# Attention kernel: a copy ahead of a softening, value products behind a second product, a fourth pair begun with the third

## The chip, the cores and the metric

The kernel runs on one core of a Trainium2 chip. The metric is device time in microseconds (us) of one execution, given as the median of several runs. Times in the text are us if nothing else is said, and times inside a stage count from the start of the profiled span.

## What is computed

The input is eight images of 256 channels and 1024 positions. The first layer is attention with eight heads; the second is attention of a token with all tokens of its image, followed by a mixture of eight experts. The change touches the attention of the second layer, for each image (batch) once:

```python
def _L1_attn_ref(x, W):                       # x: layer-normed tokens, 8 x 1024 x 256
    xa = jnp.einsum('bnd,ed->bne', x, W)
    scores = jnp.einsum('bne,bme->bnm', xa, x)
    attn = jax.nn.softmax(scores, axis=-1)
    y = jnp.einsum('bnm,bmd->bnd', attn, x)
    return y

# --- layer 0 ---
x = _L0_conv_ref(x, L0_conv_w_qkv, L0_conv_b_qkv, L0_conv_w_out, L0_conv_b_out)
# --- layer 1 ---
t = _to_tokens(x)
t = t + _L1_attn_ref(_ln_t(t), L1_attn_W)
t = t + _L1_ffn_ref(_ln_t(t), L1_ffn_router_w, L1_ffn_w1, L1_ffn_b1, L1_ffn_w2, L1_ffn_b2)
```

Layer 0 also needs, for the batch that comes next, its value projection `v` (eight blocks of 128 tokens by 512) and its first queries and keys. The kernel computes part of these inside the second layer's attention of the batch before.

## The kernel before

All work is in float32. The batches run one after the other: `layer0`, then `attend`, then routing; batches 0 to 6 are sent through their experts together, batch 7 at the end by itself (`dense`). For batch 7 `attend` runs beside the gathering of the experts' results (`others.tick`), which puts additions on DVE and transfers on the queues.

**The scores in `attend`** are a 1024 x 1024 matrix of eight row blocks of 128. They are computed by a scheme of Strassen's kind, in four pairs of row blocks: pair k makes blocks k and k + 4 with seven products of 128 x 128 by 128 x 512 in place of eight. `Pair.product` (L761) is one product, two records in the trace. Each pair has a PSUM tile of two banks (`big`, three of these in a pool): the left half `x`, the right half `v`; and one bank `z` from the pool `acc` of two banks, which the mixes' results (`py`) also use.

The steps of a pair, in the order of the program:

- `__init__`: first product into `x`; `first`, a copy of it to SBUF on ACT (L744); second product into the other half, `v`; a product into `z`; on DVE an addition of `v` (L771), which also keeps a running minimum.
- `middle`: a product accumulated into `x`; its copy `second` (L754); another one into `x`, which must wait for that copy; its copy `third` (L756); an addition of `z` on DVE.
- `rest`: two closing products, and then for the even block an addition (nmax) and the softening, an exponential on ACT over 1024 columns (L795); for the odd block a maximum on DVE (L800) and two exponentials on ACT (L804, L812). Pair 1 does the odd block first.

In the text the products of `middle` are called the pair's second and third product, as each is accumulated into `x` after the first.

**Turning and mixing.** The mix of a softened block with the tokens (`mix`, L861, 16 records of 128 x 256) needs the block transposed. `turn_now` does it on TensorE (first and last block). `turn` does it for the six others: a transpose of 32 x 32 squares on DVE (L833), and then the 16 groups of squares go to their places, eight by copies on ACT (32 x 256, L844) and eight by DMAs of 32 KB from the SP queue. The list `behind` holds back each half of them until a given copy of a later pair has been issued. `mix` ends with an addition on DVE (L870) that empties the bank `py`.

**The fill.** `fill(place)` calls `Begin.at` at named places of `attend` and of what follows (`norm 1`, `normed 1`, `last weights`, `last products`, `norm 2`, `normed 2`); each call makes one block of the next batch's value projection (`values(1)`, two products of 0.86 us in the trace's starts, L408, then a bias addition on DVE, L416). For batch 7 `fill` is another function, which does something at `last products` only.

**What sets the order.** A scheduler at build time puts each engine's instructions in a fixed order, from the program's order, the data dependencies and the `tc.issue_after` marks; it knows a PSUM tile as a whole, which is why a few places declare that there is no dependency between banks. On the chip each engine works through its list in order and waits at semaphores. The order of the program at the end of `attend` is: pairs 0 and 1 to their `middle`, `rest` of both, `turn_now` of block 0, pair 2 begun, mix 0, `middle` of pair 2, mix 1, `rest` of pair 2, pair 3 begun, mix 2, `middle` of pair 3, mix 3, `rest` of pair 3, and the mixes 4 to 7.

Of the kernel before, what the change touches and what calls it, by code (L numbers as in the profile page):

```python
# [19 lines left out]
def kernel(  # L20
# [23 lines left out]
    nc = tc.nc  # L44
# [48 lines left out]
    def acc(name):  # L93

        return ps_acc.tile([P, 512], F32, tag="acc", name=name)
# [54 lines left out]
    for e in range(E):  # L150
# [43 lines left out]
        fill=0.0,  # L194
# [135 lines left out]
    evicted = {}  # L330
# [54 lines left out]
    class Begin:  # L385
# [36 lines left out]
        def at(self, place):  # L422

            if place == "norm 1":
                self.project(True)
            elif place == "norm 2":
                with tc.issue_after(evicted["mixed"].ins):
                    self.project(True)
            self.values(1)

        def all(self):
            for _ in range(3):
# [245 lines left out]
    def attend(b, t1, fill, tick=nothing):  # L678
# [13 lines left out]
        HALF = S // 2  # L692
        xa = one.tile([P, NCC, NH2, HALF], F32, tag="xa", name=f"xa_{b}")
        mixes = one.tile([P, 7, HALF], F32, tag="res", name=f"mixes_{b}")
        b11, b12, b21, b22 = (nT[:, e, ts(n, HALF)] for e in range(2) for n in range(2))
        t1_, t2_, t3_, t4_ = (mixes[:, i, :] for i in range(4))
# [4 lines left out]
        a11, s3_, a12, a22 = (xa[:, e, n, :] for e in range(2) for n in range(2))  # L701
        s1_, s2_, s4_ = (mixes[:, 4 + i, :] for i in range(3))
# [27 lines left out]
        class Pair:  # L730

            def __init__(self, k):
                self.k = k
                both = big(f"ps1_{b}_{k}")
                self.x, v = both[:, :HALF], both[:, HALF:]
                self.z = acc(f"ps1z_{b}_{k}")
                self.ex = [homes[EX[2 * k + h]] for h in range(2)]
                self.low = [
                    small.tile([P, 1], F32, tag=f"nlow{h}", name=f"nlow_{b}_{k}_{h}")
                    for h in range(2)  # L740
                ]
                self.left = self.ex[0][:, :HALF]
                self.product(self.x, a11, b11, True)
                self.first = nc.scalar.copy(self.left, self.x)  # L744
                second = self.product(v, a12, b21, True)
                tc.declare_no_dep(second.ins, self.first.ins, reason="the other bank")
                self.product(self.z, s1_, t1_, True)
                self.add(self.left, v, 3.0e38, self.low[0])

            def middle(self, behind=None):  # L750
                far = self.ex[1][:, HALF:]
                with tc.issue_after(behind.ins) if behind else nullcontext():
                    self.product(self.x, s2_, t2_, False)
                self.second = nc.scalar.copy(self.ex[0][:, HALF:], self.x)  # L754
                self.product(self.x, s3_, t3_, False)
                self.third = nc.scalar.copy(far, self.x)  # L756
                self.add(far, self.z, 3.0e38, self.low[1])
                return self
# [23 lines left out]
            def rest(self, behind=None):  # L782
                k = self.k
                self.product(self.z, s4_, b22, False)
                self.product(self.x, a22, t4_, False)
                nmax, ssum = [], []
                for h in range(2):
                    nmax.append(small.tile([P, 1], F32, tag="nmax", name=f"nmax_{b}_{2 * k + h}"))
                    ssum.append(small.tile([P, 2], F32, tag="ssum", name=f"ssum_{b}_{2 * k + h}"))
                ex0, ex1 = self.ex  # L790

                def even():
                    tick(("max", 2 * k), self.add(ex0[:, HALF:], self.z, self.low[0], nmax[0]))
                    with tc.issue_after(behind.ins) if behind else nullcontext():
                        nc.scalar.activation(  # L795
                            ex0, ex0, AF.Exp, bias=nmax[0], scale=-1.0, accum_out=ssum[0][:, 0:1]
                        )

                def odd():
                    last = nc.vector.tensor_scalar(  # L800
                        scrap, self.x, -1.0, self.low[1], ALU.mult, ALU.min, accum_out=nmax[1]
                    )
                    tick(("max", 2 * k + 1), last)
                    nc.scalar.activation(  # L804
                        ex1[:, :HALF],
                        self.x,
                        AF.Exp,
                        bias=nmax[1],
                        scale=1.0,
                        accum_out=ssum[1][:, 0:1],  # L810
                    )
                    nc.scalar.activation(  # L812
                        ex1[:, HALF:],
                        ex1[:, HALF:],
                        AF.Exp,
                        bias=nmax[1],
                        scale=-1.0,
                        accum_out=ssum[1][:, 1:2],
                    )

                for half in (odd, even) if k == 1 else (even, odd):
                    half()
                return [(2 * k, ex0, ssum[0][:, 0:1], None), (2 * k + 1, ex1, *self.halves(ssum[1]))]
# [4 lines left out]
        def turn(i, ex, behind=None):  # L828


            at_sq, at_aT = SQ_AT[i]
            sq = homes[at_sq]
            nc.vector.transpose(sq, ex)  # L833
            if at_aT is None:
                aT = two.tile([P, S], F32, tag="tr", name=f"aT_{b}_{i}")
            else:
                aT = homes[at_aT]
            to = aT.rearrange("p (m a q) -> p a m q", a=NQ, q=SQ)
            since = sq.rearrange("p (m k q) -> p k m q", k=NQ, q=SQ)
            for a in range(NQ):  # L840
                for k in range(NQ):
                    move = nc.sync.dma_start if (a + k) % 2 else nc.scalar.copy
                    with tc.issue_after(behind[a * 2 // NQ].ins) if behind else nullcontext():
                        move(to[ts(k, SQ), a], since[ts(a, SQ), k])  # L844
            return [aT[:, ts(m, P)] for m in range(NT)]
# [10 lines left out]
        def mix(at, aT, ssum, more):  # L856
            i = BLOCKS[at]
            ahead = fill("last products") if at == NT - 1 else None
            py = acc(f"py_{b}_{i}")
            for m in range(NT):  # L860
                evicted["mixed"] = nc.tensor.matmul(  # L861
                    py[:, :D], aT[m], n1[:, m, :], start=(m == 0), stop=(m == NT - 1)
                )
            rs = small.tile([P, 1], F32, tag="rs1", name=f"rs1_{b}_{i}")
            if more is not None:
                nc.vector.tensor_add(rs, ssum, more)
                ssum = rs
            nc.vector.reciprocal(rs, ssum)
            with tc.issue_after(ahead.ins) if ahead else nullcontext():
                mixed = nc.vector.scalar_tensor_tensor(  # L870
                    t2[:, i, :], py[:, :D], rs, t1[:, i, :], ALU.mult, ALU.add
                )
            tick(("mixed", at), mixed)
# [3 lines left out]
        def turned(at, ex, ssum, more, behind=None):  # L877
            return at, turn(at, ex, behind), ssum, more

        pairs = [Pair(0).middle(), Pair(1).middle()]  # L880
        first, second = pairs[0].rest(pairs[1].third)
        second = turned(*second)
        third, fourth = pairs[1].rest()
        now = turn_now(0, first[1])
        pairs.append(Pair(2))
        mix(0, now, *first[2:])
        pairs[2].middle(evicted["mixed"])
        third = turned(*third, (pairs[2].first, pairs[2].second))
        fourth = turned(*fourth, (pairs[2].second, pairs[2].second))
        mix(*second)  # L890
        fifth, sixth = pairs[2].rest()
        pairs.append(Pair(3))
        mix(*third)
        pairs[3].middle()
        fifth = turned(*fifth, (pairs[3].second, pairs[3].second))
        sixth = turned(*sixth, (pairs[3].third, pairs[3].third))
        mix(*fourth)
# [436 lines left out]
    class Results:  # L1334
# [96 lines left out]
        def tick(self, place, behind=None):  # L1431
            added, sent, stored = self.PLACES.get(place, (0, 0, 0))
            if place == ("max", 0):
                self.scored = behind
            if added:
                with tc.issue_after(behind.ins):
                    for _ in range(added):
                        self.add()
            for _ in range(sent):
                self.gather(behind)  # L1440
            for _ in range(stored):
                if self.whole:
                    b, total, n = self.whole.pop(0)
                    store(b, total, n)
# [135 lines left out]
    for b in range(B):  # L1580
# [18 lines left out]
        def fill(place):  # L1599

            nonlocal norm
            others.tick(place)
            if place == "last products":
                norm = Norm(t1, one.tile([P, NT, D], F32, tag="xa", name=f"n2_{b}"), 1e-5, f"f{b}")
                return norm.blocks(0, NT - 1)
# [46 lines left out]
```

## Time and profile before

| | us |
|---|---|
| median of 3 runs | 2337.22 |
| lowest and highest run | 2333.23, 2338.61 |
| the profiled execution, as timed | 2328.95 |
| its span, first to last instruction | 2327.1 |
| ACT busy | 1163.0 (50%) |
| DVE busy | 1554.5 (67%) |
| mean granted TensorE clock | 0.992 |
| scores' products, L761, one record | 0.592, 448 records |
| mixes, L861, one record | 0.379, 1024 records |

The attention stage of `attend` begins at 189.4, 432.1, 672.3, 912.7, 1153.2, 1394.1, 1634.2 and about 2100 us for batches 0 to 7. The stages of batches 1 to 6 have the same order of instructions and all but the same idle times; batch 0 and batch 7 differ. Records of matmuls overlap, so that the distance between two starts says more of what a product takes than its length does: 0.86 us for a product of two records.

TensorE's idle time in these stages, by what ended it, as the trace lists it (us, times, longest):

```
PE ps L761 <- ACT home L754: 8.2, 14, 1.6
PE py L861 <- DVE t L870: 3.8, 5, 0.9
PE ps L761 <- ACT home L756: 3.4, 2, 2.8
PE ps L761 <- DVE nlow L771: 2.4, 8, 1.1
PE pa L851 <- ACT home L804: 1.7, 2, 0.9
```

A line reads: the engine and the line that waited, the tile that it writes, then the engine, tile and line that released it.

### The profile page before, as it was taken

To read this page: it belongs to the slowest core of one execution; us is meant where nothing else is said; L and a number is where in the kernel's file an instruction comes from. 1 tells how busy PE (TensorE), PEld (TensorE's weight loads), DVE (VectorE), ACT (ScalarE), POOL (GpSimd) and SP (SyncE) were. 2 spreads that over 40 slices of the span, in tenths; PEclk is the share of its full clock that TensorE was granted. 3 is DMA by queue.
4 is the path that set the end of the run, shared out by engine and by line. 5 is a ranking of instruction groups with operands and counts; after the bars stand their busy time and mean duration, and the time that the engine had idled before them with its cause. 6 is when DMAs were issued, how large, how long until landed. Compare 5 with 4: busy or idle time off the path is not lost.

```text
span 2327.1 us, 37989 instructions
## 1 busy us (share of the span) xinstructions
PE 2261.6 (97%) x13059; PEld 1216.1 (52%) x13059; DVE 1554.5 (67%) x4029; ACT 1163.0 (50%) x2138; POOL 410.7 (18%) x392
## 2 busy tenths in 40 slices
PE   9999999999999999999999999999999999998798
PEld 3345533563456335643564355435553488884565
DVE  5775687567855786578657775777568766436655
ACT  3664466456635663656365646465646622225211
POOL 0000012000200020003000200020002135545563
PEclk9999999999999999999999999999999999999899
DMA  8995201020103010201020101100111157765574
GB/s 294 385 386 154 68 17 39 9 56 13 44 2 62 8 49 1 46 19 53 3 46 19 49 8 29 36 26 13 23 42 42 49 145 192 192 199 145 154 210 113
DMA packets 278759, 200.10 MB, mean 86 GB/s; under 512 B 189576, under 2 KB 232232, under 8 KB 276776
## 3 DMA queue, kind: packets, MB, share of 16 engines
q1 hardware_dynamic: 252472, 139.14, 21.2%
q0 software_dynamic: 25008, 58.01, 7.8%
q8 instruction: 104, 1.70, 0.3%
q10 hardware_dynamic: 1088, 0.52, 0.1%
q14 instruction: 87, 0.71, 0.1%
HBM read 108.88 MB, written 110.90 MB: 94 GB/s over the span
## 4 chain that ended last, share of the span: by engine, by line
PE 80%; ACT 5%; DVE 4%; issue 4%; DMA 3%; POOL 3%; SPq 1%; another core or an unknown queue 0%; DVEq 0%; ACTq 0%; POOLq 0%
PE po L569 19%; PE psc L492 19%; PE py L861 7%; PE pqk L371 7%; PE pr L671 5%; PE pv L408 4%; PE ps L761 4%; PE ph L1269 3%; PE pe L1295 3%; PE px L708 2%; POOL yk L1391 2%; PE pqk L349 2%; PE ps1z L761 2%; DMA y<-yb 1%; ACT aT L844 1%
## 5 line engine op out<-in xcount | busy, mean ns | idle before, releaser
L533 ACT ACTIVATE ex<-psc,nmax 128x1024 f32<-128x1024 f32 x512 | 570.0, 1114 | 299.8 <-DVE scrap L516 217.4
L492 PE MATMUL psc<-qk,qk 64*64 64x512 f32 x4096 | 575.8, 593 | 3.8 <-ACT ex L533 3.5
L569 PE MATMUL po<-ex,vs 64*64 64x512 f32 x4096 | 570.6, 591 | 3.6 <-DVE vs L549 2.6
L516 DVE TENSOR_SCALAR_CACHE_REDUCE scrap<-psc,nmax 128x512 f32<-128x512 f32 x512 | 384.2, 750 | 160.3 <-PE psc L492 133.6
L507 DVE TENSOR_REDUCE nmax<-psc 128x1 f32<-128x512 f32 x512 | 350.1, 684 | 9.3 <-PE psc L492 9.3
L492 PEld LDWEIGHTS psc<-qk,qk 64*64 64x64 f32 x4096 | 180.4, 132 | 279.2 <-ACT ex L533 132.6
L569 PEld LDWEIGHTS po<-ex,vs 64*64 64x64 f32 x4096 | 176.5, 132 | 275.6 <-DVE vs L549 82.1
L1081 POOL DMA_INDIRECT rows<-n,d_at x112 | 109.0, 973 | 661.1 <-DVE nmax L507 660.8
L1008 POOL TENSOR_TENSOR t<-t,n 128x2048 f32<-128x2048 f32 x8 | 36.3, 4535 | 875.5 <-DVE n L263 875.5
L371 PE MATMUL pqk<-xT,wqkv 128*128 128x512 f32 x384 | 171.2, 599 | 0.0
L861 PE MATMUL py<-n,spare 128*128 128x256 f32 x512 | 122.0, 394 | 11.3 <-DMA out_dram<-oT 3.8
L336 ACT ACTIVATE qk<-pqk,b_qks 128x512 f32<-128x512 f32 x124 | 85.6, 690 | 86.7 <-PE pqk L371 77.6
L1391 POOL DMA_INDIRECT yk<-y,yat x112 | 111.3, 994 | 76.4 <-issue 28.4
L371 PEld LDWEIGHTS pqk<-xT,wqkv 128*128 128x128 f32 x384 | 71.0, 190 | 99.9 <-issue 77.0
L408 PE MATMUL pv<-wqkv,xT 128*128 128x512 f32 x256 | 121.5, 599 | 1.5 <-DVE v L416 1.0
L861 PEld LDWEIGHTS py<-n,spare 128*128 128x128 f32 x512 | 100.7, 198 | 38.1 <-issue 23.9
L671 PE MATMUL pr<-wo,res 128*128 128x256 f32 x512 | 111.9, 379 | 0.7 <-ACT res L588 0.7
L844 ACT COPY spare<-home 32x256 f32<-32x256 f32 x256 | 103.0, 402 | 10.0 <-DVE home L833 6.7
L671 PEld LDWEIGHTS pr<-wo,res 128*128 128x128 f32 x512 | 97.2, 190 | 17.7 <-ACT res L588 4.7
L1279 ACT ACTIVATE hb<-ph,wb 128x256 f32<-128x256 f32 x96 | 40.1, 470 | 126.9 <-issue 89.4
L533 ACT ACTIVATION_READ_ACCUMULATOR ex<-psc,nmax 128x1 f32 x512 | 99.1, 194 | 0.0
L870 DVE SCALAR_TENSOR_TENSOR t<-py,rs,t 128x256 f32<-128x256 f32 x64 | 30.5, 476 | 98.0 <-PE py L861 85.3
(256 smaller groups left out, 2939.7 us busy)
## 6 DMA issues: line engine op xcount, KB each, us to landing
rows<-wb SPq DMA_DIRECT2D x7, 8192.0 KB
xr<-rows SPq DMA_DIRECT2D x252, 64.0 KB
y<-yb POOLq DMA_DIRECT2D x63, 256.0 KB
xs<-in_x_dram SPq DMA_DIRECT2D x64, 128.0 KB
spare<-home SPq DMA_DIRECT2D x256, 32.0 KB
out_dram<-oT SPq DMA_DIRECT2D x60, 128.0 KB
xT<-in_x_dram SPq DMA_DIRECT2D x7, 1024.0 KB
sums<-t SPq DMA_DIRECT2D x7, 1024.0 KB
```

Of the source, the lines that this page charges most:

```text
L371: mm = nc.tensor.matmul(pq[:, ts(n, 512)], wqkv[:, cc, t, ts(g, P)], xT[:, cc, ts(n, 512)], start=(cc == 0), stop=(cc == NCC - 1),)
L408: nc.tensor.matmul(pv, self.xT[:, cc, ts(i, P)], wqkv[:, cc, 2, :], start=(cc == 0), stop=(cc == NCC - 1),)
L492: mm = nc.tensor.matmul(pss[at, h][ts(c, DK), ts(n, 512)], k[r, j * P + c * DK : j * P + (c + 1) * DK], q[r, ts(n, 512)], start=True, stop ...
L507: firsts[at, h] = nc.vector.tensor_reduce(nmax, pss[at, h][:, ts(0, 512)], AX.X, ALU.max, negate=True)
L516: seconds[h] = nc.vector.tensor_scalar(scrap, pss[at, h][:, ts(1, 512)], -1.0, nmaxes[at, h], ALU.mult, ALU.min, accum_out=nmax,)
L533: nc.scalar.activation(ex, pss.pop((at, h)), AF.Exp, bias=nmaxes.pop((at, h)), scale=1.0, accum_out=sums[at][:, h : h + 1],)
L569: mm = nc.tensor.matmul(po[n][ts(h, DK), :], vss[at][keys, h, :], exps[at, h][keys, ts(n, 512)], start=(j == 0 and turn == 0), stop=(j == ...
L671: nc.tensor.matmul(pr[:, :C], res[:, g, ts(i, P)], wo[:, g, :], start=(g == 0), stop=(g == NPAIR - 1))
L761: return nc.tensor.matmul(to, stationary[:, ts(self.k, P)], moving, start=start, stop=True, skip_group_check=not start,)
L844: move(to[ts(k, SQ), a], since[ts(a, SQ), k])
L861: evicted["mixed"] = nc.tensor.matmul(py[:, :D], aT[m], n1[:, m, :], start=(m == 0), stop=(m == NT - 1))
L1391: ins = nc.gpsimd.indirect_dma_start(out=self.slot(at)[:, k, :], out_offset=None, in_=self.group.y[:, :], in_offset=bass.IndirectOffsetOnAxis(
```

## The change

It has five parts. The value block made at `last products` is made at a new place, `between`, right behind the third pair's second product (for batch 7 nothing is made there). `middle` is cut in two, `middle` (second product and its copy) and `end` (third product, its copy, an addition). The fourth pair's first two products come right after the third pair is begun, before the first mix, and its copy, its bank `z` and its addition later in `open`. The softening of the second pair's even block is called only after the third pair is begun, so that the third pair's first copy is ahead of it. The third mix stands between the fourth pair's second and third product. And in the turn of block 6 two of the eight DMAs become copies on ACT, so ten copies and six DMAs.

```diff
@@ Begin.at
-            self.values(1)
+            if place != "last products":
+                self.values(1)
@@ class Pair
-                self.x, v = both[:, :HALF], both[:, HALF:]
-                self.z = acc(f"ps1z_{b}_{k}")
+                self.x, self.v = both[:, :HALF], both[:, HALF:]
...
                 self.product(self.x, a11, b11, True)
+                if k < 3:
+                    self.open()
+                else:
+                    self.product(self.v, a12, b21, True)
+
+            def open(self):
                 self.first = nc.scalar.copy(self.left, self.x)
-                second = self.product(v, a12, b21, True)
-                tc.declare_no_dep(second.ins, self.first.ins, reason="the other bank")
+                if self.k < 3:
+                    second = self.product(self.v, a12, b21, True)
+                    tc.declare_no_dep(second.ins, self.first.ins, reason="the other bank")
+                self.z = acc(f"ps1z_{b}_{self.k}")
                 self.product(self.z, s1_, t1_, True)
-                self.add(self.left, v, 3.0e38, self.low[0])
+                self.add(self.left, self.v, 3.0e38, self.low[0])
 
             def middle(self, behind=None):
+                with tc.issue_after(behind.ins) if behind else nullcontext():
+                    mm = self.product(self.x, s2_, t2_, False)
+                self.second = nc.scalar.copy(self.ex[0][:, HALF:], self.x)
+                return mm
+
+            def end(self):
                 far = self.ex[1][:, HALF:]
-                with tc.issue_after(behind.ins) if behind else nullcontext():
-                    self.product(self.x, s2_, t2_, False)
-                self.second = nc.scalar.copy(self.ex[0][:, HALF:], self.x)
                 self.product(self.x, s3_, t3_, False)
@@ Pair.rest, even
                     tick(("max", 2 * k), self.add(ex0[:, HALF:], self.z, self.low[0], nmax[0]))
+                    if k != 1:
+                        self.soften()
@@ turn
-                    move = nc.sync.dma_start if (a + k) % 2 else nc.scalar.copy
+                    away = (a + k) % 2 and (i < 6 or a > 0)
+                    move = nc.sync.dma_start if away else nc.scalar.copy
@@ attend
         now = turn_now(0, first[1])
         pairs.append(Pair(2))
+        pairs[1].soften()
+        pairs.append(Pair(3))
         mix(0, now, *first[2:])
-        pairs[2].middle(evicted["mixed"])
+        between = pairs[2].middle(evicted["mixed"])
+        with tc.issue_after(between.ins):
+            fill("between")
+        pairs[2].end()
...
         fifth, sixth = pairs[2].rest()
-        pairs.append(Pair(3))
-        mix(*third)
-        pairs[3].middle()
+        pairs[3].open()
+        between = pairs[3].middle()
+        with tc.issue_after(between.ins):
+            mix(*third)
+        pairs[3].end()
```

What the scheduler makes of it on TensorE in batches 1 to 6, from the first mix on (s2 and s3 are a pair's second and third product, z3 is the fourth pair's product into its bank z, c the two closing products of a pair, v a value product of 0.86 us, m0 to m7 the mixes, T the transposes of the last block):

```
before: m0  v s2(2) v s3(2)  m1  c(2) z3  m2 s2(3) s3(3)     m3  c(3)    m4 T v v m5 m6 m7
after:  m0  s2(2) v v s3(2)  m1  c(2) z3  s2(3) m2 s3(3)  v  m3  c(3) v  m4 T     m5 m6 m7
```

On ACT, from the second block's turn on (k the copies of 32 x 256, E the softening of the second pair's even block, f, s and t the first, second and third copy of a pair, X the exponentials of the third pair):

```
before: 8k E f(2) 4k f(3) s(2) 4k 1k t(2) 7k X s(3) 4k t(3) 4k 8k
after:  8k f(2) E 4k s(2) 4k 3k t(2) 5k f(3) X s(3) 8k t(3) 8k
```

On DVE the fourth pair's addition of `v`, which follows f(3), stands ahead of the addition that empties the bank of m1; before the change it stood earlier, ahead of the third pair's addition of `z`. In batch 0 the order after is m0 s2(2) v v s3(2) v, the closing products of the third pair, v, s2(3), s3(3), m1, z3, m2. In batch 7 the order on TensorE is the same before and after. Outside these stages no engine's order changes.

More of the change, by code (lines that the diff above doesn't have):

```diff
@@ L793, in even, with soften @@
                     tick(("max", 2 * k), self.add(ex0[:, HALF:], self.z, self.low[0], nmax[0]))
+                    if k != 1:
+                        self.soften()
+                def soften():
                     with tc.issue_after(behind.ins) if behind else nullcontext():
@@ L797, in even @@
                         )
+                self.soften = soften
                 def odd():
@@ L878, in turned @@
             return at, turn(at, ex, behind), ssum, more
-        pairs = [Pair(0).middle(), Pair(1).middle()]
+        pairs = [Pair(0)]
+        pairs[0].middle()
+        pairs[0].end()
+        pairs.append(Pair(1))
+        pairs[1].middle()
+        pairs[1].end()
         first, second = pairs[0].rest(pairs[1].third)
```

## The prediction

> **What bounds the kernel now.** I read the page's busy times first, then the timeline of one attention stage engine by engine (batch 2, 679 to 739 us; batches 1 to 6 repeat it), then the stretches' clocks.
>
> ```profile
> span 2327.1 us, 37989 instructions
> PE 2261.6 (97%) x13059; PEld 1216.1 (52%) x13059; DVE 1554.5 (67%) x4029; ACT 1163.0 (50%) x2138; POOL 410.7 (18%) x392
> ```
>
> TensorE is busy 97% of the span, so all idle time together is 65.5 us, and only idle time can be won: the edits add and remove no matrix product. TensorE's rows of the stage (start us, length us, engine, line, operation, tiles; in brackets the idle time before it and its releaser; two records are one 512-column product, sixteen are one mix):
>
> ```profile
> 700.28 1.02 PE L408 MATMUL pv<-wqkv,xT 128*128 128x512 f32 x2
> 701.50 1.12 PE L761 MATMUL ps<-mixes 128*128 128x512 f32 x2 [0.19 <-DVE nlow L771]
> 702.46 1.02 PE L408 MATMUL pv<-wqkv,xT 128*128 128x512 f32 x2
> 703.81 1.13 PE L761 MATMUL ps<-mixes,xa 128*128 128x512 f32 x2 [0.33 <-ACT home L754]
> 704.77 3.62 PE L861 MATMUL py<-n,aT 128*128 128x256 f32 x16
> ...
> 709.95 1.02 PE L761 MATMUL ps1z<-mixes 128*128 128x512 f32 x2
> ...
> 714.26 1.02 PE L761 MATMUL ps<-mixes 128*128 128x512 f32 x2
> 716.01 1.13 PE L761 MATMUL ps<-mixes,xa 128*128 128x512 f32 x2 [0.73 <-DMA home<-home]
> ```
>
> ```profile
> 728.19 3.62 PE L861 MATMUL py<-n,spare 128*128 128x256 f32 x16
> 732.45 3.69 PE L861 MATMUL py<-n,spare 128*128 128x256 f32 x16 [0.65 <-DVE t L870]
> ```
>
> Start to start, a product takes 0.86 us (709.09 to 709.95) and a mix 3.45; the first product after a wait takes 0.96 (703.81 to 704.77). By these (the brackets leave out the tail of a product's length, which the next one overlaps) the stage loses 0.36 at 701.50, 0.49 at 703.81, 0.89 at 716.01 and 0.81 at 732.45, with three restarts of 0.10 and one of 0.08. Why, is in the rows of ScalarE (ACT), VectorE (DVE) and the SP queue:
>
> ```profile
> 698.33 1.15 ACT L795 ACTIVATE home<-home,nmax 128x1024 f32<-128x1024 f32 x1
> 699.48 0.56 ACT L744 COPY home<-ps 128x512 f32<-128x512 f32 x1
> 700.89 1.65 ACT L844 COPY spare<-home 32x256 f32<-32x256 f32 x4 [0.84 <-DVE home L833]
> ...
> 703.17 0.59 ACT L754 COPY home<-ps 128x512 f32<-128x512 f32 x1
> ```
>
> ```profile
> 699.61 1.25 DVE L833 STREAM_TRANSPOSE home<-home 128x1024 f32<-128x1024 f32 x1 [3.37 <-ACT home L795]
> 700.78 0.65 DVE L771 CUSTOM_DVE_ANT_0 home<-home,ps 128x512 f32<-128x512 f32 x1
> ```
>
> ```profile
> 718.09 12.80 SPq L844 DMA_DIRECT2D spare<-home  x16
> ```
>
> The third pair's second product (701.50) waits for the add of 700.78, which waits behind a transpose, and that behind the softening of 698.33. The third product waits for the copy of 703.17. The fourth pair's third product (716.01) comes right behind its second, with only the copy between. The seventh mix (732.45) starts 1.56 us after the SP queue has issued the last of 16 DMAs (718.09 + 12.80 = 730.89); the DVE instruction that the row names empties another bank.
>
> **The change part by part,** walked through with these durations along each engine's order as built, batch 2 first.
>
> *Copy ahead of the softening.* ScalarE comes free at 698.33 as now. The copy goes first, the softening starts 0.61 later (a copy before an activation, 226.37 to 226.98 in batch 0), at 698.94; the add is done by about 699.7, so the second product starts when TensorE is free: 700.28 instead of 701.50, 0.36 of idle time gone. But the softening is 0.61 late, and its transpose (start to start 1.28) comes at 700.22, the four 32x256 copies at 701.50; they stand ahead of the pair's second copy, which starts at 703.15 (4 x 0.41) and ends at 703.73. The third product starts at 703.78, 0.03 earlier than now. The value product (1.72, both halves) now lies behind the second product and ends at 702.86, so the wait is 0.92: the stall has moved, not gone. Gain 0.03.
>
> *The new queue.* In the built order three, not one, of the next 32x256 copies precede the pair's third copy, then five more, and the first copy of the fourth pair, formerly at 702.69, comes only behind all of these: 703.76 + 4 x 0.41 + 3 x 0.41 = 706.65 third copy, 707.26 + 5 x 0.41 = 709.32 fourth pair's first copy, done 709.90. On DVE the fourth pair's add waits for it (709.94 to 710.55) and, behind that in the queue, the emptying of the second mix's bank (L870 for py_4, 708.43 now): 710.55 to 711.03. The fourth pair's third operand product (ps1z_3, 709.95 now) takes that bank. Without a wait it would start at 703.78 + 0.96 + 3.45 + 0.86 + 0.86 = 709.91; it starts at about 711.08. **New wait 1.17, with the restart 1.27.** What is late behind it: the nmax of the third pair (711.6), its softening, the fifth mix's transposes; these are needed from 724 on and ready by 722.
>
> *Fourth pair begun with the third; mix between its products.* The third mix (3.45) now lies between the fourth pair's second and third product, whose chain (1.02 + copy 0.58) is hidden under it: 0.89 + 0.10 gone. If that mix were not there the 0.99 would be back.
>
> *Value products.* Two single products take places behind the third and fourth pairs instead of before the sixth mix: same 1.72 us, no cost, but they no longer cover the wait for the seventh mix's turned block.
>
> *Two DMAs become two copies in that turn.* ScalarE does 10 x 0.41 = 4.1 us instead of 3.3; the SP queue issues 6 instead of 8 (5.2 us now from 725.7 to 730.89, 0.65 each). In the walk TensorE has the fourth pair's closing products at 721.54, the fifth mix at 724.12, the seventh mix at 731.89. The softening starts at 723.39, the transpose at 724.95 behind the bias addition of the value product, the copies at 726.2 to 730.3, the DMAs land at 726.2 + 6 x 0.65 + 1.56 = 731.7. No wait, slack 0.2: 0.89 gone. With eight DMAs there would be one of 1.1.
>
> Batch 2: -0.03 - 0.99 - 0.89 + 1.27 = **-0.64**; the next stage's first product starts at 738.79 instead of 739.43. Batch 1 gives -0.67. In batches 3 to 6 the wait before the seventh mix is 0.90 where it is 0.65 here, but the landing is 0.26 later too and eats the slack: -0.8 each. Together -4.5; bounds: nothing won at the seventh mix, -4.5 + 5.3 = +0.8; new wait half as long, -4.5 - 3.8 = -8.3.
>
> *Batch 0* is ordered differently: the fourth pair's second and third product come before the second mix. The same walk gives waits of 0.92, 1.68, 1.49, 0.83 and 0.79, with restarts 6.4, where the trace has 5.1 in the same places (0.19 to 1.56 shown, plus restarts). **+1.3**, bounds 0 and +2.
>
> *Batch 7* has no value products. Its second copy, bound by the queue of ScalarE, comes at 2130.58 for 2130.08: +0.5. Its last turned block's eight DMAs are issued in 8.95 us, 1.12 each, and TensorE idles 2.17 before the seventh mix; two fewer save between 0 and 2.2. I take 1.0, as in batch 2 most but not all of the 1.3 is won. **-0.5**, bounds -1.7 and +0.5.
>
> Sum: -4.5 + 1.3 - 0.5 = **-3.7 us.** The profiled execution took 2328.95 (span 2327.1), so 2325.2 for one like it; it is 8.3 below the median of the runs shown, 2337.22 (2333.23 to 2338.61). Against the median: **2333.5**, -0.16%.
>
> One possible cost, the clock. Batch 0 idles 1.56 us before a product, and its stretch keeps clock 1.00 (last but two columns: PEclk, DMA share, GB/s follow the busy times):
>
> ```profile
> 222.00:228.00 6.00, 3.87 (x10) 1.25 (x9) 2.12 (x6) 5.81 (x13) 0.00 (x0) 1.00 0.32 51
> ...
> 2130.00:2140.00 10.00, 8.89 (x25) 5.42 (x24) 8.42 (x22) 6.58 (x15) 6.03 (x6) 0.83 0.80 204
> ```
>
> In batch 7 the stretch behind idle times of 1.05 and 0.68 has 0.83, which costs 10 x 0.17 = 1.7 us. I take the first: the new waits are of its size. By the row of batch 7 seven stages would cost 12 us and the sum would be +8. [...]
>
> **The rivals.** (1) *The new wait is shorter or absent*, because the bank is freed earlier than walked (DVE's add takes the copy sooner, the small copies overlap). For: the walk chains 21 ScalarE instructions, and 0.05 too much in each is 1.0. Against: the queues are in order, and 0.41 is steady over all 256 of them. Half gone: -7.5, 2329.7; all: -11.3, 2325.9. (2) *The gain at the seventh mix doesn't come*: another DMA, or the ten copies, land last. Slack is 0.2, so 0.25 us on the landing removes a part and 1.1 the whole: -3.7 + 5.3 = +1.6, 2338.8; half, 2336.2. (3) *Slower*: the new wait at ps1z_3 is longer. Without it batches 1 to 6 win 12.1, batches 0 and 7 lose 0.8; at 1.9 us with restart per batch nothing is left, from 2.7 it is slower by 0.2%. If the emptying of the bank came also behind the third pair's nmax and maximum (0.75 + 0.75 on DVE), it is 2.8: +5.5, 2342.7. For: it stands in the same queue; against: in the built order these two come behind it. (4) The change doing nothing is excluded, as the built order differs in every stage.
>
> **How the numbers follow.** A measurement of this kernel can tell about 0.2% (4.7 us) from no change. Forecast 0.60, its own range 2330 to 2337 with the spread of the runs (2.7 either way); rival 1 0.20, rival 2 0.10, rival 3 0.10. The forecast lies 1 us inside the bound, so of its 0.60 some 0.20 falls beyond it; rival 1 is faster nearly whole: faster 0.40, same 0.49 (0.40 + 0.09 of rival 2), slower 0.11. The range reaches to rival 1's full case and half way to rival 3: 2326.5 to 2340.
>
> **What would show it.** Behind the first mix, the second product without idle time and the third with about 0.9. ps1z_3 with 1.2 of idle time before it, released by DVE L870 of the changed numbering. No idle time between the fourth pair's second and third product, none before the seventh mix. Batch 0 longer by 1.3. Wrong it would be if ps1z_3 starts without a wait, or if the seventh mix still waits for DMAs.

## The result and the profile after

The changed kernel took 2333.59 us (median of 12, 2330.56 to 2340.12), the kernel before beside it 2335.81 (median of 12, 2333.16 to 2338.61): a ratio of 0.9991 with a 95% interval of 0.9982 to 1.0001. That is no change that can be told. The whole of the two profiled spans says the same, 2328.6 for 2327.1, but its stages do not. A stage's length is taken here from the first record of the `px` products of a batch to the first record of what follows the attention, read from the starts in the timelines (the second set is one of the sets of runs below, made on another chip):

```
batch                      0      1      2      3      4      5      6      7   1 to 6
before                 69.26  67.13  67.10  67.36  67.36  67.13  67.92  87.70   404.00
changed                72.64  66.77  66.68  66.70  66.71  66.68  67.69  86.87   401.23
before, second set     69.27  67.14  67.11  67.37  67.37  67.15  67.05  81.09   403.19
changed, second set    70.97  66.79  66.69  66.71  66.70  66.69  67.23  81.95   400.81
```

Batches 1 to 6 won 2.77, batch 7 0.83; batch 0 lost 3.38, and the stretches between the stages, which the change doesn't touch, took 1.73 more in this execution (2.23 of it behind batch 7). So the gain was not won and lost in one place: it is small in each of six stages, and one stage gives it back.

TensorE's timeline of batch 2 in the changed kernel (start, length, engine, line, operation, tiles; in brackets the idle time before and its releaser):

```profile
703.36 1.02 PE L772 MATMUL ps<-mixes 128*128 128x512 f32 x2
704.21 1.88 PE L408 MATMUL pv<-wqkv,xT 128*128 128x512 f32 x4
706.89 1.12 PE L772 MATMUL ps<-mixes,xa 128*128 128x512 f32 x2 [0.79 <-ACT home L761]
...
712.16 1.02 PE L772 MATMUL ps<-mixes,xa 128*128 128x512 f32 x2
714.25 1.13 PE L772 MATMUL ps1z<-mixes 128*128 128x512 f32 x2 [1.06 <-DVE t L887]
...
719.52 1.02 PE L772 MATMUL ps<-mixes,xa 128*128 128x512 f32 x2
...
731.59 7.19 PE L878 MATMUL py<-n,spare 128*128 128x256 f32 x32
```

The wait before the third pair's second product is gone, the one before its third product has grown (706.89 - 704.21 - 1.72 = 0.96 with the tail of the product before), the fourth pair's third product (719.52) has none, the seventh mix has 0.13 (731.59 to the start of the eighth is 7.03, two mixes are 6.90). New is `ps1z_3` at 714.25: 714.25 - 712.16 - 0.86 = 1.23. ScalarE and VectorE, in the same kernel, show why:

```profile
710.38 2.08 ACT L861 COPY spare<-home 32x256 f32<-32x256 f32 x5
712.48 0.58 ACT L750 COPY home<-ps 128x512 f32<-128x512 f32 x1
```

```profile
713.10 0.69 DVE L782 CUSTOM_DVE_ANT_0 home<-home,ps 128x512 f32<-128x512 f32 x1 [2.02 <-ACT home L750]
713.71 0.08 DVE L782 DVE_READ_ACCUMULATOR2_ANT nlow<- 128x1 f32 x1
713.71 0.48 DVE L887 SCALAR_TENSOR_TENSOR t<-py,rs,t 128x256 f32<-128x256 f32 x1
```

Five small copies stand ahead of the fourth pair's first copy, the add waits 2.02 for it, and the emptying of the second mix's bank (713.71) only stands behind that add: the mix had ended before 711.5. The list of TensorE's waits (total, times, longest) has it six times, once in each of batches 1 to 6:

```profile
PE ps1z L772 <- DVE t L887: 6.4, 6, 1.1
```

Batch 0 of the changed kernel, first TensorE, then the clock by stretches of 2 us (the columns of busy time of PE, PEld, DVE, ACT and POOL, then the granted clock, DMA share and GB/s):

```profile
228.66 1.12 PE L772 MATMUL ps<-mixes 128*128 128x512 f32 x2 [1.27 <-DVE nlow L782]
230.49 1.97 PE L772 MATMUL ps<-mixes,xa 128*128 128x512 f32 x2 [0.71 <-ACT home L761]
232.25 4.51 PE L878 MATMUL py<-n,aT 128*128 128x256 f32 x16
```

```profile
230.00:232.00 2.00, 1.51 (x2) 0.73 (x3) 0.32 (x2) 0.44 (x1) 0.00 (x0) 0.66 0.05 7
232.00:234.00 2.00, 2.00 (x6) 1.36 (x5) 0.00 (x0) 0.58 (x1) 0.00 (x0) 0.50 0.03 8
```

The product takes 1.76 start to start (230.49 to 232.25) instead of 0.96, the mix 4.35 (to 236.60) instead of 3.45: 1.70 of the 3.38 is the clock. The rest is longer waits: with the tails they sum to 6.02 (0.96, 1.72, 1.43, 0.87, and 1.04 before `pa`), where the kernel before has 4.35.

### The profile page after: what moved, and what is told of

It is laid out like the page before. It is cut to its first block, busy times and chain, and to the rows that moved or that the text cites. A ratio compares the mean times of both kernels' runs of the same rounds, so it can differ in the third digit from the quotient of the medians.

```text
span 2328.6 us, 37960 instructions
## 1 busy us (share of the span) xinstructions
PE 2258.4 (97%) x13059; PEld 1217.2 (52%) x13059; DVE 1556.0 (67%) x4029; ACT 1171.3 (50%) x2154; POOL 409.0 (18%) x392
## 4 chain that ended last, share of the span: by engine, by line
PE 81%; ACT 5%; DVE 4%; DMA 3%; issue 3%; SPq 2%; POOL 1%; another core or an unknown queue 1%; DVEq 0%; ACTq 0%; POOLq 0%
PE po L570 19%; PE psc L493 19%; PE pqk L371 7%; PE py L878 6%; PE pr L672 5%; PE pv L408 4%; PE ph L1298 3%; PE pe L1324 3%; PE ps L772 3%; PE pdh L1547 2%; PE pdy L1571 2%; PE px L709 2%; PE pqk L349 2%; SPq L861 2%; PE ps1z L772 1%
## 5 line engine op out<-in xcount | busy, mean ns | idle before, releaser
L861 ACT COPY spare<-home 32x256 f32<-32x256 f32 x272 | 109.4, 402 | 15.5 <-DVE home L849 10.5
```

## The experiments

Twelve kernels ran in three sets, each set on a chip of its own; the kernel before took 2318.65, 2317.39 and 2330.83 beside them. So times are compared as ratios within a set, and stages by their length, which in batches 1 to 6 hardly differs between chips (the table above).

**The emptying ahead of the add** (first set):

```diff
-                self.add(self.left, self.v, 3.0e38, self.low[0])
+                with tc.issue_after(evicted["emptied"].ins) if self.k == 3 else nullcontext():
+                    self.add(self.left, self.v, 3.0e38, self.low[0])
...
+            evicted["emptied"] = mixed
```

> The changed kernel with one order turned round on VectorE: the emptying of the second mix's bank now stands ahead of the fourth pair's add (in batches 1 to 6 nothing else moves; in batch 0 the scheduler also puts the second mix ahead of the fourth pair's second product). Theory: the 1.06 us before ps1z_3 is a queue, the emptying is ready when the mix ends (about 711.5 in batch 2) but waits behind the add, which waits for the late copy. Then ps1z_3 starts right behind the product before it, and the stages of batches 1 to 6 (66.7 us each) get shorter by 0.9 to 1.2 each, 5.4 to 7.2 in all; ps1z_3 leaves the list of waits. Rival: TensorE comes 1.2 earlier to the seventh mix, whose turned block had only 0.1 of slack, and waits there for the transfers instead: stages shorter by under 0.3, the idle time now before the seventh mix. Second rival: the bank is not what ps1z_3 waits for, and the wait stays. Batch 0: with fewer waits in a row no stretch under a clock of 0.9, 3 to 5 us shorter than 72.6.

Ratio 0.9943 (0.9926 to 0.9959). Batches 1 to 6 took 65.4 to 66.0, 394.17 in all: 6.6 to 7.1 less than the changed kernel in its two profiles (and 6.5 less than the next kernel, on the same chip). TensorE and VectorE of batch 2:

```profile
706.64 1.02 PE L773 MATMUL ps<-mixes,xa 128*128 128x512 f32 x2
707.50 1.02 PE L773 MATMUL ps1z<-mixes 128*128 128x512 f32 x2
```

```profile
705.98 0.48 DVE L888 SCALAR_TENSOR_TENSOR t<-py,rs,t 128x256 f32<-128x256 f32 x1 [0.42 <-PE py L879]
707.58 0.69 DVE L783 CUSTOM_DVE_ANT_0 home<-home,ps 128x512 f32<-128x512 f32 x1 [1.11 <-ACT home L750]
```

The emptying now runs as soon as the mix ends, and `ps1z_3` follows its predecessor after 0.86 without a wait. The theory holds: the wait was a place in a queue, not work. The second rival falls. A piece of the first is there: batches 3 and 5 show 0.41 and 0.32 of idle time before the seventh mix and won 0.7 and 0.8 in place of 1.3, but most of the gain stayed. Batch 0 took 68.24.

**Batch 0 in the order of the others** (first set):

```diff
+                with tc.issue_after(evicted["mixed"].ins) if k == 2 else nullcontext():
+                    self.product(self.z, s4_, b22, False)
+                    self.product(self.x, a22, t4_, False)
...
-        between = pairs[3].middle()
+        between = pairs[3].middle(evicted["mixed"])
```

> The changed kernel with batch 0 put in the order of the other batches (both value products and the second mix ahead of the fourth pair's second and third product); batches 1 to 6 are built as in the changed kernel. Theory: batch 0 lost 3.4 us by its own order, 1.7 by longer waits and 1.7 by the clock that fell to 0.72 behind them. In the new order it should take 66.7 to 68.5 (72.64 in the changed kernel, 69.26 before), without a stretch below 0.9 of the clock; batches 1 to 6 as they are, 66.7 each; whole kernel 4 to 6 us under the changed kernel. Rival: the low clock has nothing to do with the order (it falls in that place of the run anyway): then batch 0 gains only the waits, 1.5 to 3 us, and the stretch behind 230 us still shows 0.7 to 0.8.

Ratio 0.9960 (0.9946 to 0.9974). Batch 0 took 65.85, better than expected; batches 1 to 6 400.65, unchanged. Behind 220 us one wait of 0.80 and one of 0.38 are left, and the clock stays:

```profile
226.00:230.00 4.00, 4.00 (x14) 2.35 (x13) 2.51 (x7) 2.13 (x4) 0.00 (x0) 1.00 0.34 55
230.00:236.00 6.00, 6.00 (x26) 4.49 (x25) 3.86 (x9) 5.86 (x17) 0.00 (x0) 1.00 0.18 29
```

The waits of batch 0 come from its order. Whether the clock does, the next runs had to say.

**Eight DMAs again** (first set):

```diff
-                    away = (a + k) % 2 and (i < 6 or a > 0)
+                    away = (a + k) % 2
```

> The changed kernel with the last turned block moved by eight DMAs and eight copies again instead of six and ten; nothing else differs in any order. Theory (the prediction's): the seventh mix waits for the last DMA, and two DMAs fewer won 1.1 per batch; the wait returns with 1.0 to 1.3 in batches 1 to 6, their stages take 67.6 to 67.9 instead of 66.7, in all 6 to 8 us more, and batch 7 1 to 2 more. Rival: the copies of ScalarE or the emptying of a bank end last there, and the wait stays at 0.1, the stages at 66.7. Batch 0 is built as in the changed kernel: if the clock falls to about 0.7 again behind 230 us, that belongs to its order and not to one execution.

2330.27 in one run. Batches 1 to 6 took 67.6 to 68.0, 406.67 in all, 5.4 to 5.9 more than the changed kernel in its two profiles and 6.0 more than the kernel above (400.65), on the same chip; and the wait before the seventh mix is back (batch 2):

```profile
732.79 3.62 PE L878 MATMUL py<-n,spare 128*128 128x256 f32 x16
737.29 3.69 PE L878 MATMUL py<-n,spare 128*128 128x256 f32 x16 [0.89 <-DVE t L887]
```

737.29 - 732.79 - 3.45 = 1.05: two DMAs are worth 1.0 per batch, as the prediction has it. The wait is new in batch 0 too (1.19 shown), which took 72.39. But the four waits before, the same as in the changed kernel, left the clock at 1.00 here. Batch 7 took 0.8 more than in the kernel above, under the 1 to 2 expected.

**The softening first again** (first set):

```diff
-                    if k != 1:
-                        self.soften()
-
-                def soften():
                     with tc.issue_after(behind.ins) if behind else nullcontext():
                         nc.scalar.activation(
...
-                self.soften = soften
...
-        pairs[1].soften()
```

> The changed kernel with only its first part undone: the softening stands ahead of the third pair's first copy again. By the walk of the prediction the second product then waits 1.2 (it has no value product ahead of it any more), but the softening, its transpose and the small copies come 0.6 earlier, the third product waits no more, and the chain to ps1z_3 is 0.65 shorter, so that its wait falls from 1.2 to 0.2 to 0.4: stages of batches 1 to 6 66.0 to 66.6 instead of 66.7, so the copy ahead of the softening is worth nothing or costs up to 0.7 per batch. Rival (the copy is what the change wins by): the wait before the second product comes on top of the others, stages of 67.2 to 68. Batch 0: the clock again 0.7 to 0.8 behind 230 us if its waits stay as long; 1.00 if the sum of waits falls under that of the kernel before.

2314.24 in one run, where the kernel before took 2318.65. Stages of 66.17 to 66.25 in batches 1 to 5 and 66.73 in batch 6, 397.66 in all. Batch 2:

```profile
701.91 1.12 PE L772 MATMUL ps<-mixes 128*128 128x512 f32 x2 [1.05 <-DVE nlow L782]
702.88 1.88 PE L408 MATMUL pv<-wqkv,xT 128*128 128x512 f32 x4
704.59 1.02 PE L772 MATMUL ps<-mixes,xa 128*128 128x512 f32 x2
...
711.08 1.12 PE L772 MATMUL ps1z<-mixes 128*128 128x512 f32 x2 [0.29 <-DVE t L882]
```

The wait moves from the third to the second product and grows a little (1.21 for 0.96, tails included), and the one before `ps1z_3` shrinks from 1.06 to 0.29: the first part of the change costs 0.5 per batch as it stands. Batch 0 here has 3.6 of idle time shown.

**The changed kernel again, and the kernel before** (second set, unaltered).

> The changed kernel itself once more, unaltered, on the chip of the other runs. Theory: batch 0's waits are fixed by its order and come again (0.8, 1.6, 1.3 and 0.7 shown), but the clock of 0.5 to 0.7 behind 230 us, which a kernel with the same order and the same waits did not show, does not belong to them: batch 0 then takes 70.9 to 71.2 instead of 72.64. Rival: the clock falls there whenever those waits come: 72.6 again, with a stretch of 0.7. Batches 1 to 6 66.7 each in both. Ratio to the kernel before 0.997 to 1.000.

> The kernel before once more, unaltered, on the chip of the other runs, for stages to compare on one chip: batches 0 to 6 as in its first profile (69.26, 67.1 to 67.4, 67.9), since waits inside the core set them; batch 7 and the end shorter than 87.7 and 125.4 if it is the memory side that makes this chip faster (theory), all stages shorter in proportion if it is a clock (rival).

Ratio 0.9998 (0.9988 to 1.0007), as in the first measurement. Batch 0 took 70.97; its waits are the same to 0.01, its clock is not:

```profile
230.00:232.00 2.00, 1.46 (x5) 0.93 (x6) 0.32 (x2) 0.78 (x3) 0.00 (x0) 1.00 0.07 10
232.00:234.00 2.00, 2.00 (x11) 1.77 (x10) 0.00 (x0) 0.29 (x1) 0.00 (x0) 1.00 0.04 8
```

So the waits cost 1.70 each time (70.97 - 69.27), the clock another 1.70 in the first profile and nothing in this one. The kernel before differs from its first profile in batch 7 (81.09 for 87.70), behind it (134.9 for 139.7 from that stage's end to the end of the span) and in batch 6 (67.05 for 67.92), not in batches 0 to 5. So no clock shortens all stages alike, and the rival is out; that it is the memory side is not shown by this.

**The second copy ahead of four small ones** (second set):

```diff
-        third = turned(*third, (pairs[2].first, pairs[2].second))
+        third = turned(*third, (pairs[2].second, pairs[2].second))
```

> The changed kernel with one edit: the four small copies that stood between the third pair's softening and its second copy now come behind the second copy (the scheduler then puts seven between second and third copy, nine behind the third, and on VectorE of batches 1 to 6 the emptying of the second mix's bank ahead of the fourth pair's add). Theory: the 0.8 to 0.9 before the third pair's third product is those copies ahead of one that TensorE waits for, and the wait before ps1z_3 is the place behind the add; both go, and the stages of batches 1 to 6 take 64.3 to 65.0 instead of 66.7, 10 to 14 us in all. Rival: what is won comes back before the seventh mix, which has 0.1 of slack: 65.4 and more, with 0.5 to 1.0 of idle time there. Second rival: the third copy, behind seven small copies, makes the next product wait: idle time before ps1z_2 or the one behind it.

Ratio 0.9956 (0.9941 to 0.9971); batches 1 to 6 65.1 to 65.8, 392.05 in all, 8.8 to 9.2 less. As the scheduler also put the emptying ahead of the add, this run joins that order with the new one. Both waits are gone, but the stages miss the expected 64.3 to 65.0: batch 2 shows a wait that neither rival named, before the fourth pair's second product:

```profile
711.45 1.13 PE L772 MATMUL ps<-mixes 128*128 128x512 f32 x2 [0.56 <-DVE nlow L782]
```

It is the add (from 710.70), behind the fourth pair's first copy (from 710.08), behind nine small ones (from 706.32). Batches 3, 5 and 6 also show 0.16 to 0.54 of idle time before the seventh mix, the first rival in part. Batch 0 took 72.24, with waits of 2.29 and 1.25, and the clock at 0.63 and 0.52 in the two stretches behind 230 us.

**Three orders mended, then four** (second and third set). The first joins the three edits above (copy, emptying, batch 0). The second, in place of the mark on the emptying, takes the fourth pair's first copy and its add between the transpose of the fourth block and that block's small copies (`take` is a method that makes this copy and this add):

```diff
+            behind = behind() if callable(behind) else behind
...
-        fourth = turned(*fourth, (pairs[2].second, pairs[2].second))
+        fourth = turned(*fourth, pairs[3].take)
```

> The changed kernel with three orders mended: second copy ahead of the four small ones, emptying of the bank ahead of the add, batch 0 in the order of the others. Theory: the gains add, batch 0 64 to 65 (65.85 with its order alone), batches 1 to 6 64.3 to 65.0 each, whole kernel 17 to 22 us under the kernel before, ratio 0.990 to 0.993. Rival: the seventh mix's transfers become the bound and take 0.5 to 1.0 per batch back: ratio 0.993 to 0.995, no better than the emptying alone (0.9943).

> The version with three orders mended and a fourth: the fourth pair's first copy comes behind the third copy and one small copy, no longer behind nine small ones. Theory: the 0.56 us of idle time left before the fourth pair's second product (with the tail of a product and the restart 0.73 to 0.82) is that copy and the add behind it; it goes, the stages of batches 1 to 6 take 64.2 to 64.5 instead of 65.1, the kernel 4 to 6 us less: ratio 0.988 to 0.991. Rival: TensorE then runs into the seventh mix's transfers: 0.4 to 0.8 of idle time there, stages 64.8 to 65.1, ratio as with three orders (0.9917).

Three: ratio 0.9917 (0.9903 to 0.9930), as expected, but batch 0 took 65.60 and batches 1 to 6 65.0 to 65.6, 391.08 in all, at or above the upper end of what was expected; the 0.56 is still there. In batches 1 to 6 the gains don't add, as the run before had the emptying ahead of the add already (392.05). Four: ratio 0.9888 (0.9870 to 0.9906), 2306.25 for 2330.83; batch 0 65.60, batches 1 to 6 64.3 to 64.5, 386.39 in all. TensorE's batch 2 with four shows no wait from the first mix to the pair's last product:

```profile
702.37 1.02 PE L778 MATMUL ps1z<-mixes 128*128 128x512 f32 x2
703.22 1.02 PE L778 MATMUL ps<-mixes 128*128 128x512 f32 x2
704.08 3.62 PE L886 MATMUL py<-n,spare 128*128 128x256 f32 x16
707.54 1.02 PE L778 MATMUL ps<-mixes,xa 128*128 128x512 f32 x2
...
719.61 7.32 PE L886 MATMUL py<-n,spare 128*128 128x256 f32 x32
```

What is left is before the seventh mix: 726.77 - 719.61 - 6.90 = 0.26, restart included. This version is faster than the kernel before by 1.1% (0.9 to 1.3), and so than the changed kernel, whose own ratios are 0.9991 and 0.9998.

**Four, and the softening first in batch 7 alone** (third set):

```diff
-                    if k != 1:
+                    if k != 1 or b == B - 1:
...
-        pairs[1].soften()
+        if b < B - 1:
+            pairs[1].soften()
```

> As the version with four orders mended, and in batch 7 alone the softening ahead of the third pair's first copy again. With only that part undone batch 7 took 78.5 us, against 82.0 in the changed kernel and 81.1 before. Theory: batch 7 has no value product to cover the late second copy (2.5 us of idle time, and a slow clock behind it), so the order of before is better there: batch 7 1 to 3 us shorter than with four orders mended, all else equal. Rival: the 78.5 came from transfers and clock of that one execution: no difference beyond 1 us.

Ratio 0.9894 (0.9878 to 0.9911), median 2306.04: not distinguishable from 0.9888. Batch 7's stage is 83.27 for 87.80 in the two profiles, but in the medians nothing comes of it. Two profiles of one kernel, on two chips, differ by 5 to 7 us there (the table above), so one profile each can't settle an effect of 1 to 3: it stays open.

**The value products back, the mix outside** (third set):

```diff
-            if place != "last products":
+            if place != "between":
```

> The changed kernel with the block of value products that it puts behind the third pair's second product back at the place before the last mixes. In the built order one of the two halves stays behind that product, one goes behind the fourth pair's third product, two behind the last transposes; the scheduler also puts the emptying of the bank ahead of the add. Walk: 0.86 less to cover the third product's wait, which grows from 0.9 to 1.8; the wait before ps1z_3 goes (-1.27); none before the seventh mix. Stages of batches 1 to 6: 66.7 + 0.86 - 1.27 = 66.3, so the moved products are a cover worth 0.86 and no more. Rival: the cover is not used (the second copy ends earlier when the rest is earlier): 65.4; or the wait before ps1z_3 stays: 67.5.

2333.43 in one run, where the kernel before took 2330.83. Stages of 67.73, a miss. The two waits are as walked (1.66 shown before the third product, none before `ps1z_3`). But the scheduler also put the fourth pair's closing product ahead of the fourth mix, right behind a value product, and it waits for the third copy there (1.30 shown):

```profile
722.21 1.02 PE L408 MATMUL pv<-wqkv,xT 128*128 128x512 f32 x2
724.53 1.13 PE L772 MATMUL ps<-mixes,xa 128*128 128x512 f32 x2 [1.30 <-ACT home L767]
```

724.53 - 722.21 - 0.86 = 1.46, with the restart 1.56, and 66.26 + 1.56 is 67.8. The run shows what the cover is worth at the third product (0.86), not what the moved products are worth alone. Batch 0 took 74.70, with a wait of 2.72 and a clock of 0.50 behind it.

```diff
-        between = pairs[3].middle()
-        with tc.issue_after(between.ins):
-            mix(*third)
+        mix(*third)
+        pairs[3].middle()
```

> The changed kernel with the third mix ahead of the fourth pair's second product instead of between its second and third; in the built order a value product (0.86) then stands between the two. The prediction holds that without the mix the 0.99 is back: 67.7 for the stages of batches 1 to 6. Rival: the value product covers the copy (0.58 and some 0.1 of hand-over) as well: 66.7 to 66.9, and the mix was not needed for it; the gain came from any work put between the two.

2328.26 in one run, where the kernel before took 2330.83. Stages of 67.0 to 67.3: between the two. The rival is right on the spot (batch 2):

```profile
718.33 1.02 PE L408 MATMUL pv<-wqkv,xT 128*128 128x512 f32 x2
719.18 1.10 PE L772 MATMUL ps<-mixes,xa 128*128 128x512 f32 x2
```

No wait between second and third product with only a value product between. Of the 0.56 (67.25 - 66.69) some 0.09 is lost by that product, which takes 0.95 (719.18 to 720.13), and 0.48 before the seventh mix, where 0.37 of idle time is shown; why the mix waits there is not shown. Batch 0, in the order of the changed kernel, kept the clock: its product at 230.42 took 0.96 and the mix behind it 3.46, where the changed kernel's first profile has 1.76 and 4.35.

## Why the prediction was right, and where it was off

The forecast, 2333.5 and no change that can be told, was met (2333.59), and so was its kind of reason: a small gain in each of six stages, the larger part of it eaten by a new wait, and a loss in batch 0. That the median agrees to 0.1 is luck. The forecast takes 3.7 off 2337.22, the median of three runs; the twelve runs of the kernel before that belong to the result have 2335.81, so the measured difference is 2.2, and its interval includes no change. In the profiled pair the span grew by 1.5 where 3.7 less was forecast: batches 1 to 6 won 1.7 less, batch 0 lost 2.1 more, the stretches between the stages, booked at nothing, took 1.7 more, and batch 7 won 0.3 more.

- *The third pair.* Second product without a wait, third with 0.92: shown, 0.96. That the copy ahead of the softening wins nothing was right; undone, it gives 0.5 back, by way of `ps1z_3`, where the prediction had booked its lateness.
- *The new wait* of 1.17 at `ps1z_3`, by late copy, add and emptying in one queue: shown in all six batches, 1.23 in batch 2, and taken away by that order alone. Rivals 1 and 3 are out.
- *The seventh mix.* Gain by two DMAs fewer: shown (1.0 by undoing it). The slack of 0.2 was mis-sized: a wait of 0.13 is left in batch 2, and batch 6 shows 0.90 in the first profile and 0.42 in the second. Rival 2 is out, though a piece of it is here.
- *Batches 1 to 6*, -4.5: measured -2.8 and, in the second set, -2.4. In batch 2 it is -0.42 instead of -0.64: 0.04 at the third product, 0.06 at `ps1z_3`, 0.13 at the seventh mix. The step "-0.8 each" for batches 3 to 6 fails most. It rests on a wait of 0.90 before the seventh mix, which the kernel before has in batches 3 and 4 alone; batch 5 has 0.68, and batch 6 1.47 or, in the second set, 0.59. Batches 3 and 4 won 0.66, batch 5, whose stage before was as short as batch 2's, 0.45, and batch 6 0.23, or lost 0.18.
- *Batch 0*, +1.3: the five waits (0.92, 1.68, 1.49, 0.83, 0.79) came as 0.96, 1.72, 1.43, 0.87 and 1.04, and cost 1.70 against before. Taking the clock at no cost failed in the recorded execution, another 1.70. The rival row, batch 7's, was the right one to fear, but for one stage and not for seven.
- *Batch 7*, -0.5: its parts are seen (third product 0.5 later behind the mix; the wait before the seventh mix 0.90 for 2.17, and 0.18 for 0.89 in the second set), but the stage went -0.83 and +0.86. The sum is not decided.
- *"If that mix were not there the 0.99 would be back"*: wrong for this order, since a value product covers the same copy; what is lost is 0.56, most of it before the seventh mix. With no work at all between the two products it wasn't run.

## What to carry to other kernels

When a copy is moved ahead on one engine, follow every queue behind it to the next instruction that TensorE needs: here the stall went through a row of small copies on ScalarE into VectorE's queue, and came out at a bank that had long been ready to empty. An instruction whose input is ready belongs ahead of one that still waits; a few such changes of order, no work saved, were worth 1.1%, where the change itself was worth nothing that can be told. A stage built in another order than its sisters (batch 0) has to be walked by itself.

## What the hardware showed unexpectedly

The clock fell behind idle times none of which was longer than 1.56, and not each time. Four executions had the order of the changed kernel in batch 0 up to 236 us, with idle times shown of 0.8, 1.6, 1.3 and 0.7 within ten us: one fell to 0.50, three kept 1.00. Both executions with one idle time above 2.2 there (2.29 and 2.72) fell; but in batch 7 of the changed kernel a product behind an idle time of 2.33 ran at full speed (0.96 to the next). A fall in batch 0 lasted 3.41 us in the changed kernel's first profile, where it cost 1.70; by the clocks of the 2 us stretches it lasted 3.4 with the wait of 2.29 and 6.8 with that of 2.72.

What sorts these cases is not shown. Ahead of the fall in the changed kernel's first profile, and in it:

```profile
227.23:230.64 3.41, 1.43 (x4) 0.45 (x4) 2.45 (x10) 3.08 (x7) 0.00 (x0) 1.00 0.30 47
230.64:234.05 3.41, 3.41 (x7) 2.00 (x8) 0.00 (x0) 0.58 (x1) 0.00 (x0) 0.50 0.02 5
```

TensorE is busy for 1.43 of the 3.41 us ahead, and in the next 3.41 the clock is 0.50. But between 226 and 230 us the two profiles of the changed kernel hardly differ, with TensorE busy for 2.51 of 4.00 us in the first and 2.57 in the second, and behind this the clock is 0.50 in one and 1.00 in the other. Nor does a fall need idle time right ahead of it: behind batch 7's stage the kernel before has TensorE busy all through 2216.08 to 2219.50, at a clock of 1.00, and 0.50 from there to 2222.91. That several short waits close together add up was the author's estimate; nothing was varied on purpose to test it.
